# Attention block with adjacency mask on one core: exponentials issued behind each step's piece, half of the mask written by ScalarE, the last tail in halves

## The chip, the cores and the metric

One of the eight cores of a Trainium2 chip. The time is device microseconds of the slowest (here the only) core. Kernels are compared by the ratio to runs of the kernel before on the same chip.

In the profile's lines PE is TensorE (matrix products), PEld its weight loads, DVE is VectorE, ACT ScalarE, POOL GpSimd and SP SyncE. The kernels put TensorE's results into tiles of their PSUM pools, here called banks; an accumulating DMA is a transfer that a kernel issues with accum_op=ALU.add, to add to what stands at its target. A line of a wait list says who waited, in which line of the kernel, for whom: us in all, times, longest. One fp32 matmul of the program is two in the profile's counts (the values' four matmuls a step are 8192 records in 1024 steps); a transpose is one (four of them are an x4).

## The reference, cut to what matters

```python
# x: (8, 2048, 256) fp32; adj: (2048, 2048) int32, about 0.8% ones; H = 8 heads of D = 32
q, k, v = split(x @ w_qkv)                       # per frame f
scores = einsum("fnhd,fmhd->fhnm", q, k) / sqrt(32)
scores = where(adj > 0, scores, -1e9)
t = softmax(scores) @ v
y = layernorm(x + t) ; y = layernorm(y + relu(y @ w1 + b1) @ w2 + b2)   # with gains and shifts
out = layernorm(x + y)
```

## The kernel before

The loop has 1024 steps: 8 frames, 4 query blocks of 512, 2 groups of 4 heads, 16 key blocks of 128. A step makes the scores of the step two ahead (four 32-row matmuls side by side), VectorE adds the mask while copying them out of PSUM, ScalarE takes the exponential, and TensorE multiplies the current step's exponentials with the values.

```python
for t, (f, qc, g, mb) in enumerate(items):
    ...
    if mb:
        advance(t, 1)                    # one "piece" of other work that needs a PSUM bank
    scores(items[t + 2])                 # TensorE, then two VectorE additions
    values(items[t])                     # TensorE
    exponentials(items[t + 2])           # ScalarE, 128x2048
    add_up(items[t])                     # sums of exponentials: GpSimd or accumulating DMAs
```

Everything else (turning x, projections, closing sums, norms and the feed-forward of blocks already finished) is cut into pieces, at most one a step. The kernel uses eight banks of PSUM: six hold score pairs, one collects the group's output, and one is left for all pieces:

```python
def bank(...):
    if state["side"] is not None:
        return ps_x[1 - state["side"]].tile(...)      # in the loop: always the same one
    ...                                               # outside: five to choose from

def turn_rows(xc, xT):
    for a in range(2):
        yield BANK                                    # waits for the next step
        ps = bank()
        ... four transposes into ps
        nc.scalar.copy(xT[:, a, :], ps)               # ScalarE, behind exponentials(t + 1)
```

The masks are made before the loop: VectorE casts a chunk of adj to 0 or -57344, TensorE transposes it, VectorE writes it as fp8 in two halves. After the loop, the last block's sums, division, norms and feed-forward run alone.

## Time and profile before

| | us |
|---|---|
| median of the runs beside the changed kernel | 3594.7 (3592.2 to 3596.2) |
| start of the loop (masks, first projections) | 99.9 |
| loop, from its first scores to the end of the last values | 3417.4 |
| tail | 73.5 |
| TensorE idle in the loop | 304.1 |

The three stages are read from the records: the loop starts at the first scores after the mask stage and ends with the last values matmul.

### The profile page before, as it was taken

How to read it: one execution, taken by the hardware profiler on the slowest of the kernel's cores; microseconds unless marked ns; L12 is line 12 of the kernel's file. 1: busy time of each engine (PE TensorE's matmuls, PEld its weight loads, DVE VectorE, ACT ScalarE, POOL GpSimd, SP SyncE). 2: the span in 40 equal slices, each digit the busy share in tenths (PEclk: the TensorE clock that was granted, in tenths of full speed). 3: DMA queues.
4: the chain of work that ended last, by engine and by line, in shares of the span. 5: the costliest groups of instructions: out<-in, count | busy, mean ns of one | idle time of the engine just before them, and what ended most of it. 6: DMA issues, size and time to landing. Idle time of an engine off the chain costs nothing. (4 is left out here: it accounts for less than half of the span.)

```text
span 3590.9 us, 54434 instructions
## 1 busy us (share of the span) xinstructions
PE 3199.5 (89%) x22020; PEld 1036.2 (29%) x22020; DVE 2745.6 (76%) x3191; ACT 2413.7 (67%) x1921; POOL 2628.5 (73%) x1399
## 2 busy tenths in 40 slices
PE   6889998899988999998989999999998999988884
PEld 4222332223322233222322223222232223322221
DVE  5788768886788867877778776887768877688882
ACT  2576667776677766777677676677667776677772
POOL 3577768787688766878677776787767877688885
PEclk8999999999999999999999999999999999999997
DMA  8677768778578767778667778677776778587763
GB/s 300 138 157 159 171 149 179 153 152 187 130 158 188 154 155 154 155 165 186 156 143 163 158 159 183 131 165 172 156 178 144 151 163 176 137 170 161 152 143 73
DMA packets 146226, 576.52 MB, mean 161 GB/s; under 512 B 14608, under 2 KB 63248, under 8 KB 96816
## 3 DMA queue, kind: packets, MB, share of 16 engines
q0 software_dynamic: 66960, 443.19, 61.0%
q1 hardware_dynamic: 78192, 128.48, 10.5%
q8 instruction: 174, 2.85, 0.3%
q10 hardware_dynamic: 816, 1.31, 0.1%
q14 instruction: 84, 0.69, 0.1%
HBM read 132.52 MB, written 37.75 MB: 47 GB/s over the span
## 5 line engine op out<-in xcount | busy, mean ns | idle before, releaser
L213 DVE TENSOR_TENSOR p<-s,mask 128x1024 f32<-128x1024 f32 x2048 | 2410.2, 1219 | 697.8 <-PE s L210 409.0
L217 ACT ACTIVATE p<-p 128x2048 f32<-128x2048 f32 x1024 | 1957.4, 1911 | 1059.0 <-DVE p L213 820.4
L249 POOL TENSOR_TENSOR p<-p 128x2048 f32<-128x2048 f32 x384 | 1858.4, 4888 | 423.6 <-ACT p L217 421.6
L210 PE MATMUL s<-qT,kT 32*128 32x512 f32 x8192 | 1171.0, 641 | 169.3 <-DVE p L213 165.1
L229 PE MATMUL x<-p,v 128*32 128x512 f32 x8192 | 1092.9, 606 | 0.0
L246 POOL DMA_DIRECT2D p<-p x384 | 385.3, 1022 | 362.3 <-ACT p L217 149.9
L210 PEld LDWEIGHTS s<-qT,kT 32*128 32x128 f32 x8192 | 320.3, 183 | 797.9 <-DVE p L213 648.5
L229 PEld LDWEIGHTS x<-p,v 128*32 128x32 f32 x8192 | 161.3, 108 | 778.5 <-issue 544.1
L267 ACT ACTIVATE y<-y,nb,rs 128x256 f32<-128x256 f32 x384 | 224.9, 589 | 37.8 <-POOL nb L264 37.8
L283 PE MATMUL x<-p,ones 128*32 128x512 f32 x2048 | 243.9, 594 | 2.7 <-POOL p L249 1.2
L167 PE MATMUL x<-in,wqkv 128*128 128x512 f32 x472 | 234.0, 618 | 13.8 <-ACT turned L331 7.8
L256 DVE BATCH_NORM_STATS2 st<-y 128x6 f32<-128x256 f32 x384 | 160.0, 417 | 24.9 <-DMA y<-in_x_dram 24.9
L341 PE MATMUL x<-turned,w1s 128*128 128x512 f32 x256 | 130.6, 633 | 21.3 <-ACT hT L342 20.4
L167 PEld LDWEIGHTS x<-in,wqkv 128*128 128x128 f32 x472 | 79.9, 189 | 174.2 <-issue 71.7
L351 PE MATMUL x<-w2s,hT 128*128 128x256 f32 x512 | 127.6, 392 | 2.6 <-ACT hT L342 1.8
L192 PE MATMUL x<-wqkv,in 128*128 128x128 f32 x896 | 114.9, 281 | 7.2 <-ACT kT L169 7.0
L192 PEld LDWEIGHTS x<-wqkv,in 128*128 128x128 f32 x896 | 104.2, 191 | 55.9 <-ACT kT L169 38.3
L351 PEld LDWEIGHTS x<-w2s,hT 128*128 128x128 f32 x512 | 92.0, 189 | 66.6 <-ACT hT L342 29.4
L283 PEld LDWEIGHTS x<-p,ones 128*32 128x32 f32 x2048 | 63.4, 110 | 163.7 <-issue 124.4
L261 POOL TENSOR_TENSOR rs<-rs,mhalf 128x4 f32<-128x4 f32 x96 | 99.5, 1036 | 8.0
L330 PE MATMUL x<-ident,y 128*128 128x128 f32 x256 | 47.7, 297 | 53.2 <-ACT turned L331 37.7
L358 POOL TENSOR_TENSOR y<-y,be2r 128x1024 f32<-128x1024 f32 x32 | 94.2, 2943 | 0.2
(89 smaller groups left out, 1401.0 us busy)
## 6 DMA issues: line engine op xcount, KB each, us to landing
p<-p POOLq DMA_DIRECT2D x384, 1024.0 KB, 9.8
y<-in_x_dram POOLq DMA_DIRECT2D x64, 512.0 KB, 6.2
mask<-md SPq DMA_DIRECT2D x248, 128.0 KB, 5.7
in<-xd SPq DMA_DIRECT2D x59, 512.0 KB, 7.3
p<-in_adj_dram SPq DMA_DIRECT2D x16, 1024.0 KB, 15.4
out_dram<-y SPq DMA_DIRECT2D x32, 512.0 KB, 4.7
in<-in_x_dram SPq DMA_DIRECT2D x28, 512.0 KB, 5.6
xd<-in SPq DMA_DIRECT2D x28, 512.0 KB, 8.9
```

What stands on the lines that cost most here:

```text
L167: nc.tensor.matmul(ps, wqkv[:, a, k0:k0 + P], xT[:, a, :], start=(a == 0), stop=(a == 1))
L192: nc.tensor.matmul(ps[:, j * P:(j + 1) * P], xT[:, a, j * P:(j + 1) * P], wqkv[:, a, 2 * C + g * P:2 * C + (g + 1) * P], start=(a == 0), s ...
L210: nc.tensor.matmul(ps2[half][:, j, :], KT[f, mb // TPC, g][r:r + D, (mb % TPC) * P:(mb % TPC + 1) * P], QT[f, qc, g][r:r + D, :], start=Tr ...
L213: nc.vector.tensor_tensor(pt[:, 2 * half:2 * half + 2, :], ps, MK[f, qc, mb // 2][:, mb % 2, None, :].to_broadcast([P, 2, CH]), ALU.add)
L217: nc.scalar.activation(PT[item], PT[item], AF.Exp, scale=1.0 / math.sqrt(D))
L229: nc.tensor.matmul(O[grp][r:r + D, :], V[f, mb // TPC, g][:, mb % TPC, r:r + D], PT[item][:, h, :], start=(mb == 0), stop=(mb == LAST))
L246: nc.gpsimd.dma_start(PT[f, qc, g, chain[0]], PT.pop(item), accum_op=ALU.add)
L249: nc.gpsimd.tensor_tensor(first, first, PT.pop(item), ALU.add)
L256: nc.vector.bn_stats(st, t[:, j, :])
L267: nc.scalar.activation(t[:, j, :], t[:, j, :], AF.Identity, bias=nb[:, j:j + 1], scale=rs[:, j:j + 1])
L283: nc.tensor.matmul(ps[r:r + D, :], cst["ones"], term[:, h, :], start=(n == 0), stop=(n == 3))
L351: nc.tensor.matmul(ps[:, (j - jj) * C:(j - jj + 1) * C], hT[:, d, j * P:(j + 1) * P], w2s[:, d, :], start=(d == 0), stop=(d == 1))
```

## The change

It has three parts. The exponential of the next step is issued after this step's piece and before the scores, so that the copy that empties the pieces' bank stands ahead of it in ScalarE's queue. ScalarE writes half of each mask chunk. The last block gets its own tail: it works in halves, adds x by VectorE and not by DMA, may use five banks, and its last two tiles of exponentials go into the closing sum on TensorE and not through GpSimd. Besides, the stores of the masks and of the first turned x are issued by SyncE and no longer by GpSimd.

```diff
-            nc.vector.tensor_tensor(m, ps, ones, ALU.min, saturate=False)
-            nc.gpsimd.dma_start(MD[qc, k], words(m))
+            if half:
+                nc.vector.tensor_tensor(m, ps, ones, ALU.min, saturate=False)
+            else:
+                nc.scalar.copy(m.bitcast(I8), ps)         # -5 as int8 is -57344 as fp8
+            nc.sync.dma_start(MD[qc, k], words(m))
...
-            nc.vector.tensor_scalar(cv, col, 0.0, MASKED, op0=ALU.is_le, op1=ALU.mult)
+            for half, what in enumerate((CODE, MASKED)):
+                ... the same on half of the columns
...
         if mb:
             advance(t, 1)
+        if t + 1 < len(items):
+            exponentials(items[t + 1])
         ... scores(items[t + LEAD])
         values(items[t])
-        if t + LEAD < len(items):
-            exponentials(items[t + LEAD])
         add_up(items[t])
...
+    ENDED = (13, 15)                  # of the last group: not added by GpSimd, but terms of the sum
+    def finish(f, qc):                # the last block's tail
+        yield from divide(f, qc, y)
+        nc.vector.tensor_tensor(y, y, xr, ALU.add)        # x loaded 8 steps before the end
+        norm_halves(y) ; ... feed_forward(y) ; norm_halves(z)
+        ... gain and shift + x by VectorE, in halves
+        norm_halves(z) ; two output DMAs
...
     t = len(items)
+    state["side"] = None              # five banks from here on
```

More of the change, by code (lines that the diff above doesn't have):

```diff
@@ L13 @@
 I32 = mybir.dt.int32
+I8 = mybir.dt.int8
 F8 = mybir.dt.float8e5
@@ L31 @@
 MASKED = -57344.0
+CODE = -5.0
 BIG = 2.0 ** 64
@@ L126, in mask_blocks @@
             m = to[half] if to else mask_piece(0, qc, k)
-            nc.vector.tensor_tensor(m, ps, cst["ones"][:, 0:1, None].to_broadcast([P, 2, CH]), ALU.min, saturate=False)
-            nc.gpsimd.dma_start(MD[qc, k], words(m))
+            if half:
+                nc.vector.tensor_tensor(m, ps, cst["ones"][:, 0:1, None].to_broadcast([P, 2, CH]), ALU.min, saturate=False)
+            else:
+                nc.scalar.copy(m.bitcast(I8), ps)
+            nc.sync.dma_start(MD[qc, k], words(m))
     def load_mask(f, qc, k):
@@ L246, in add_up @@
                 nc.gpsimd.dma_start(PT[f, qc, g, chain[0]], PT.pop(item), accum_op=ALU.add)
-        if mb in POOLED[1:]:
+        if mb in POOLED[1:] and not ((f, qc, g) == items[-1][:3] and mb in ENDED):
             first = PT[f, qc, g, POOLED[0]]
@@ L275, in denominator @@
         terms = [PT.pop((f, qc, g, ALONE))] + [PT.pop((f, qc, g, chain[0])) for chain in MOVED + (POOLED,)]
+        if (f, qc, g) == items[-1][:3]:
+            terms[3:3] = [PT.pop((f, qc, g, b)) for b in ENDED]
         yield BANK
@@ L282, in denominator @@
                 r = D * h
-                nc.tensor.matmul(ps[r:r + D, :], cst["ones"], term[:, h, :], start=(n == 0), stop=(n == 3))
+                nc.tensor.matmul(ps[r:r + D, :], cst["ones"], term[:, h, :], start=(n == 0), stop=(n == len(terms) - 1))
         dT = op.tile([P, CH], F32, name="dT")
@@ L299, in denominator @@
             begin = items.index((f, qc, g, LAST)) + SUM + 2
-            start(begin, outcome(f, qc), begin)
+            start(begin, outcome(f, qc) if (f, qc) != (F - 1, NCK - 1) else finish(f, qc), begin)
     def outcome(f, qc):
@@ L304, in outcome, with divide @@
         state["tails"] += 1
-        rc = RC.pop((f, qc))
         xin = x[f, qc * CH:(qc + 1) * CH, :].rearrange("(p j) c -> p j c", p=P)
         y = yp.tile([P, TPC, C], F32, name="y")
+        yield from divide(f, qc, y)
+        nc.gpsimd.dma_start(y, xin, accum_op=ALU.add)
+        begin = items.index((f, qc, 1, LAST)) + SUM + 2
+        start(begin + 10, tail(f, qc, y, xin), begin + 26)
+    def divide(f, qc, y):
+        rc = RC.pop((f, qc))
         for gg in range(2):
@@ L316, in outcome @@
                                     rc[:, :, 4 * gg:4 * gg + 4, None].to_broadcast([P, TPC, 4, D]), ALU.mult)
-        nc.gpsimd.dma_start(y, xin, accum_op=ALU.add)
-        begin = items.index((f, qc, 1, LAST)) + SUM + 2
-        start(begin + 10, tail(f, qc, y, xin), begin + 26)
     def tail(f, qc, y, xin):
         yield from norm(y)
+        yield from feed_forward(y)
+        yield 1
+        z = y
+        yield from norm(z)
+        nc.gpsimd.tensor_tensor(z, z, rows(cst["g2r"]), ALU.mult)
@@ new lines, in tail, with norm_halves @@
+        yield 1
+        nc.gpsimd.tensor_tensor(z, z, rows(cst["be2r"]), ALU.add)
+        yield 1
+        nc.gpsimd.dma_start(z, xin, accum_op=ALU.add)
+        yield 7
+        yield from norm(z)
+        nc.sync.dma_start(out[f, qc * CH:(qc + 1) * CH, :].rearrange("(p j) c -> p j c", p=P), z)
+        state["tails"] -= 1
+    def norm_halves(t):
+        both = []
+        for h in range(0, TPC, 2):
+            mv = small.tile([P, 2, nc.vector.BN_AGGR_DIM], F32, name="mv")
+            for j in range(2):
+                st = small.tile([P, nc.vector.BN_STATS_DIM], F32, name="st")
+                nc.vector.bn_stats(st, t[:, h + j, :])
+                nc.vector.bn_aggr(mv[:, j, :], st)
+            rs = small.tile([P, 2], F32, name="rs")
+            nc.gpsimd.tensor_scalar(rs, mv[:, :, 1], EPS, 1.0, op0=ALU.add, op1=ALU.mult)
+            nc.gpsimd.tensor_tensor(rs, rs, cst["mhalf"][:, 0:2], ALU.pow)
+            nb = small.tile([P, 2], F32, name="nb")
+            nc.vector.scalar_tensor_tensor(nb, mv[:, :, 0], -1.0, rs, op0=ALU.mult, op1=ALU.mult)
+            both.append((h, rs, nb))
+        for h, rs, nb in both:
+            for j in range(2):
+                nc.scalar.activation(t[:, h + j, :], t[:, h + j, :], AF.Identity, bias=nb[:, j:j + 1], scale=rs[:, j:j + 1])
@@ new lines, in finish @@
+    def finish(f, qc):
+        y = yp.tile([P, TPC, C], F32, name="y")
+        xr, xb = state["rows"], take([P, TPC, C], F32)
+        yield from divide(f, qc, y)
+        nc.vector.tensor_tensor(y, y, xr, ALU.add)
+        norm_halves(y)
+        nc.vector.tensor_tensor(xb, xr, rows(cst["be2r"]), ALU.add)
+        yield from feed_forward(y)
+        z = y
+        norm_halves(z)
+        for h in range(0, TPC, 2):
+            nc.vector.tensor_tensor(z[:, h:h + 2], z[:, h:h + 2], rows(cst["g2r"])[:, h:h + 2], ALU.mult)
+            nc.vector.tensor_tensor(z[:, h:h + 2], z[:, h:h + 2], xb[:, h:h + 2], ALU.add)
+        norm_halves(z)
+        dst = out[f, qc * CH:(qc + 1) * CH, :].rearrange("(p j) c -> p j c", p=P)
+        for h in range(0, TPC, 2):
+            nc.sync.dma_start(dst[:, h:h + 2], z[:, h:h + 2])
@@ L323, in tail, with feed_forward @@
+    def feed_forward(y):
         yield TURNED
@@ L353, in tail @@
             nc.vector.tensor_tensor(z[:, jj:jj + 2, :], ps.rearrange("p (b c) -> p b c", c=C), z[:, jj:jj + 2, :], ALU.add)
-        yield 1
-        yield from norm(z)
-        nc.gpsimd.tensor_tensor(z, z, rows(cst["g2r"]), ALU.mult)
-        yield 1
-        nc.gpsimd.tensor_tensor(z, z, rows(cst["be2r"]), ALU.add)
-        yield 1
-        nc.gpsimd.dma_start(z, xin, accum_op=ALU.add)
-        yield 7
-        yield from norm(z)
-        nc.sync.dma_start(out[f, qc * CH:(qc + 1) * CH, :].rearrange("(p j) c -> p j c", p=P), z)
-        state["tails"] -= 1
     fill = []
@@ L425, in begin @@
             cv = two[:, c % 2 * TPC * CH:(c % 2 + 1) * TPC * CH].rearrange("p (j m) -> p j m", m=CH)
-            nc.vector.tensor_scalar(cv, col, 0.0, MASKED, op0=ALU.is_le, op1=ALU.mult)
+            for half, what in enumerate((CODE, MASKED)):
+                part = slice(half * 2 * P, (half + 1) * 2 * P)
+                nc.vector.tensor_scalar(cv[:, :, part], col[:, :, part], 0.0, what, op0=ALU.is_le, op1=ALU.mult)
             fetch()
@@ L430, in begin @@
                 yield from turn_rows(rows[c][:, 0:2, :].rearrange("p a (b c) -> p (a b) c", c=C), xT)
-                nc.gpsimd.dma_start(XD[0][c], xT)
+                nc.sync.dma_start(XD[0][c], xT)
                 XT[0, c] = xT
@@ L444, in begin @@
                     scores(items[k])
-                    exponentials(items[k])
+                exponentials(items[0])
     def ask(f, c):
@@ L465, in fast_path @@
                 start(t, what(f + 1, *which), due)
+        if t == len(items) - MB // 2:
+            state["rows"] = take([P, TPC, C], F32)
+            nc.sync.dma_start(state["rows"], x[f, qc * CH:(qc + 1) * CH, :].rearrange("(p j) c -> p j c", p=P))
         if mb:
             advance(t, 1)
+        if t + 1 < len(items):
+            exponentials(items[t + 1])
         if t + LEAD < len(items):
```

## The prediction

> **What bounds the kernel now.** I read the page's busy table first, then busy time by stage, then TensorE's waits inside the main loop, then the timeline of a stretch where it waits, and last the two ends. The table names TensorE, and the stage table (core: length, then busy us and instruction count of PE, PEld, DVE, ACT, POOL, then clock, DMA share, GB/s) says where it isn't bound:
>
> ```profile
> PE 3199.5 (89%) x22020; PEld 1036.2 (29%) x22020; DVE 2745.6 (76%) x3191; ACT 2413.7 (67%) x1921; POOL 2628.5 (73%) x1399
> ...
> 0.00:100.00 100.00, 63.42 (x476) 47.65 (x476) 60.96 (x53) 20.06 (x29) 31.97 (x54) 0.80 0.76 280
> 100.00:3518.00 3418.00, 3113.93 (x21463) 978.40 (x21464) 2670.02 (x3084) 2379.72 (x1867) 2565.70 (x1315) 1.00 0.73 160
> 3518.00:3591.00 73.00, 22.15 (x86) 10.12 (x85) 14.58 (x54) 13.88 (x26) 30.82 (x31) 0.66 0.19 45
> ```
>
> So there is a start of 100 us (the masks), a loop of 3418 us with 1024 steps in which TensorE is busy 91%, and a tail of 73 us. A loop step is: one "piece" of other work (a projection, a transpose, a part of the tail of an earlier block), the scores two steps ahead, then this step's values. The wait list of TensorE from 150 to 3500 us accounts for almost all of its 298 us of idle time there (3350 us less 3051 busy); columns are total us, times, longest:
>
> ```profile
> PE s L210 <- DVE p L213: 160.2, 347, 1.1
> PE x L147 <- ACT in L148: 40.9, 28, 2.0
> PE x L330 <- ACT turned L331: 36.5, 30, 1.4
> PE x L341 <- ACT hT L342: 19.0, 30, 1.0
> PE x L290 <- ACT dT L285: 16.0, 63, 0.5
> PE x L167 <- ACT turned L331: 7.8, 13, 0.7
> ```
>
> The first line is the steps without a piece: two score-plus-mask additions of VectorE (1.22 us each) take longer than scores plus values (1.14 + 1.06 us). All the others are one thing: a piece waits until ScalarE has copied the previous piece out of the only bank that pieces have. With four smaller ScalarE lines (7.0, 3.8, 3.2, 0.3) they sum to 134.5 us. The timeline shows why the copy is late (start us, length us, engine, line, what):
>
> ```profile
> 1907.06 0.81 PE L330 MATMUL x<-ident,y 128*128 128x128 f32 x4
> ...
> 1908.59 1.91 ACT L217 ACTIVATE p<-p 128x2048 f32<-128x2048 f32 x1 [1.10 <-DVE p L213]
> 1908.88 1.06 PE L229 MATMUL x<-p,v 128*32 128x512 f32 x8
> ...
> 1910.41 0.76 ACT L331 ACTIVATE turned<-x,be1c,g1c 128x512 f32<-128x512 f32 x1
> 1911.22 0.66 PE L330 MATMUL x<-ident,y 128*128 128x128 f32 x4 [1.28 <-ACT turned L331]
> ```
>
> The first transposes end at 1907.87, but ScalarE stands before an exponential that can only start at 1908.59 (it waits for VectorE) and lasts 1.91 us. The copy starts at 1910.41, 2.5 us after its data; TensorE loses 1.28 us.
>
> At the two ends, the second half of the mask stage and the chain of work that ended last:
>
> ```profile
> 72.09 1.22 DVE L426 TENSOR_SCALAR p<-p 128x2048 bf16<-128x2048 int32 x1
> 73.36 1.89 PE L124 MATMUL s<-identb,p 128*128 128x128 bf16 x16 [2.73 <-DVE p L426]
> 74.43 2.36 DVE L127 TENSOR_TENSOR in<-s,ones 128x1024 fp8e5<-128x1024 bf16 x2 [1.13 <-PE s L124]
> 76.71 1.22 DVE L426 TENSOR_SCALAR p<-p 128x2048 bf16<-128x2048 int32 x1
> ```
>
> ```profile
> 3519.48 4.55 POOL p L249
> 3530.73 5.54 DMA y<-in_x_dram
> 3572.16 5.58 DMA y<-in_x_dram
> ```
>
> One mask chunk takes 4.61 us, all of it VectorE (1.22 + 2.36) and a 1.13 us wait for the transposes. The tail is one serial chain with two accumulating DMAs in it.
>
> [...]
>
> **The change, part by part.**
>
> *Exponentials.* The step used to issue piece, scores(t+2), values(t), exp(t+2); now piece, exp(t+1), scores(t+2), values(t). The order listing of the built kernels confirms that on ScalarE each copy now stands before an exponential instead of behind it. No work is added or removed in the loop. In the example the copy would run at about 1907.9 to 1908.7, long before TensorE wants the bank at 1909.9. So up to 134.5 us go. I checked from the records whether VectorE lets TensorE use it: in the 219 steps with such a wait, I took the time from the end of the addition that frees the score bank to the start of the scores, less the wait: 0.82 us on average, 0.17 after the turn transposes, 0.26 after the tail's transposes, 1.56 after the feed-forward. Nearly every wait is recoverable. I take off 20 us for three things: transposes in the same step as a normalization put 0.76 + 0.59 + 1.91 = 3.26 us on ScalarE in a step of 0.66 + 1.14 + 1.06 less overlap, about 2.8 us, with some 1 us of slack before the values; GpSimd, already 75% busy in the loop, holds p buffers, and VectorE's additions already wait 33 us for buffers (behind GpSimd and DMA); and a norm's scale from GpSimd now has one exponential less to hide behind (in the loop only 3 of the norms would have been late, 2.4 us in all). Gain 115 us.
>
> *Masks.* The cast is cut into two of 128x1024, so about 0.65 us each; the first half is copied by ScalarE (about 1.05 us, from 0.59 for 512 elements), leaving one 1.22 us VectorE operation of two. Chain per chunk: 0.65 cast, then both transposes at the slow clock (1.89), 0.1 latency, 1.22 last VectorE op: about 3.9 us in place of 4.61. Over the last 8 chunks that is 5.6 us; the first 8 are held by TensorE, ScalarE copies and adjacency loads and gain little. I take 5 us. The DMAs moved to SyncE's queue are off the path.
>
> *Tail* (T is the last values' end, 3517.3). Two GpSimd additions of 4.55 us leave the chain, but 16 sum matmuls of 0.12 us come in and all 48 run after the last feed-forward piece: 2.0 + 48 x 0.116 = T+7.6, against T+7.8 before. No gain. From there: with five banks to choose from, reciprocal and both divisions end at about T+11.4 (T+12.8 before), and x is added from SBUF by an addition of 1.22 us instead of a DMA: T+12.9 with the queue's small operations, against T+19.0, gain 6.1. First norm and feed-forward: halves start ScalarE earlier and the copies no longer wait for banks (0.8 to 0.9 us, three times), but the matmuls stay at the slow clock: 21.7 us in place of 24.5, gain 2.8. Second norm, gain and shift: 4.5 + 4 x 0.69 = 7.3 us in place of 17.0 (two 2.34 us GpSimd operations and a 6 us DMA), gain 9.7. Last norm: finished after 5.7 us, but the order listing puts the previous block's last norm behind it on VectorE, GpSimd and ScalarE: 4.4 + 2.1 + 2.1 + 2.1 = 10.8 us to the end of ScalarE, against 6.3 before: loss 4.5. Sum 14 us.
>
> Total 115 + 5 + 14 = 134 us: 3595 - 134 = 3461 us.
>
> **Rivals.** (1) The wait moves to values waiting for exponentials, since exp(t+1) now stands behind a copy that waits for its piece. For it: in steps without a piece, values start only 0.99 us after their exponential ends, at the least 0.20. Against: after a piece with a copy there were 1.7 to 3.6 us on average. It would cost 30 to 60 us: about 3505. (2) VectorE becomes the bound and eats the gain, since its wait is already the largest. Against: the slack above. It would leave half: about 3525. (3) GpSimd or its accumulating DMAs (9.8 us to landing) hold buffers longer than the shorter steps allow. GpSimd would go from 75 to 78%; it sits idle 406 us waiting for exponentials. 10 to 30 us: about 3480. (4) Everything is recovered, and the clock stays up in the tail: about 3435.
>
> **Range and chances.** Rivals 1 and 3 in part give the upper end, 3505; full recovery the lower, 3435. Within 2% means above 3523, which needs the loop's gain to be less than about half; slower would need a new wait that the trace gives no hint of.
>
> **What would show it.** Right: TensorE's waits on ScalarE in the loop shrink from 134 us to under 20, its busy time in the loop stays near 3114 us, its wait on VectorE stays near 160 to 180 us, the mask chunk takes about 3.9 us, no DMA of x in the final chain, and the last ScalarE work belongs to the older block's norm. Wrong: a new line of values waiting for the exponential, or VectorE's wait growing by what ScalarE's lost, or VectorE's additions waiting for GpSimd for far more than 33 us.

## More of the kernel before

"Half clock" is a granted TensorE clock of 0.50 in the trace, full clock one of 1.00.

## The result

The changed kernel took 3439.9 us (3433.6 to 3453.0, four runs) against 3594.7, ratio 0.9575 with an interval of 0.9546 to 0.9603: 155 us won where 134 were forecast, inside the range. A ratio is the mean time of one kernel's fast runs over that of the other's of the same rounds, so it is not quite the ratio of the medians quoted.

The busy table and the three stages of the changed kernel (core: length, then busy us and count of PE, PEld, DVE, ACT, POOL, clock, DMA share, GB/s):

```profile
PE 3179.1 (92%) x22036; PEld 1038.5 (30%) x22036; DVE 2731.0 (79%) x3203; ACT 2426.5 (71%) x1937; POOL 2586.7 (75%) x1357
...
0.00:92.84 92.84, 63.45 (x472) 47.83 (x472) 43.85 (x53) 34.37 (x45) 6.75 (x19) 0.83 0.82 291
92.84:3385.61 3292.77, 3094.87 (x21460) 979.91 (x21460) 2666.88 (x3084) 2377.57 (x1867) 2561.08 (x1313) 1.00 0.76 166
3385.61:3440.00 54.39, 20.75 (x106) 10.80 (x104) 20.26 (x67) 14.56 (x26) 18.82 (x25) 0.75 0.19 45
```

| | before | after | won | forecast |
|---|---|---|---|---|
| start | 99.9 | 92.8 | 7.1 | 5 |
| loop | 3417.4 | 3292.8 | 124.6 | 115 |
| tail | 73.5 | 53.5 | 20.0 | 14 |

The stages are those of the two profiled executions, which lie 151.8 us apart; the medians lie 154.8 us apart.

**The loop.** What TensorE waits for in the loop of the changed kernel, whole list (total us, times, longest):

```profile
PE s L215 <- DVE p L218: 173.2, 358, 1.5
PE x L172 <- DMA in<-xd: 14.1, 8, 3.1
PE x L234 <- ACT p L222: 2.3, 2, 1.7
PE s L215 <- DVE in L130: 1.3, 1, 1.3
PE x L172 <- ACT turned L395: 0.3, 1, 0.3
```

Every wait of a piece for a ScalarE copy is gone but 0.3 us. The wait for VectorE has grown from 163.8 us (same bounds) to 173.2, and one of 1.2 us has become 14.1: projections that wait for reloaded inputs. TensorE's idle time fell by 106.2 us, from 304.1 to 197.9 (length less busy, both loops). The other 18.4 us of the 124.6 are busy time: 3113.3 before, 3094.9 after, for the same matmuls. (TensorE ran at half clock for two stretches of 3.41 us in the loop before and for one after; I estimate that this is 1.6 of the 18.4 us, from a later run with five more such stretches and 8.1 us more of busy time.) The timeline of two transpose pieces, as in the stretch shown of before:

```profile
1829.46 0.66 PE L394 MATMUL x<-ident,y 128*128 128x128 f32 x4
...
1830.28 0.76 ACT L395 ACTIVATE turned<-x,be1c,g1c 128x512 f32<-128x512 f32 x1
...
1830.99 1.91 ACT L222 ACTIVATE p<-p 128x2048 f32<-128x2048 f32 x1
...
1832.11 0.66 PE L394 MATMUL x<-ident,y 128*128 128x128 f32 x4
```

The copy starts at 1830.28, 0.16 us after its transposes end at 1830.12, and the exponential follows it. The next transposes start without a wait; the two pieces are 2.65 us apart, where they were 4.16 us apart before.

**The start.** One mask chunk of the second half:

```profile
69.69 1.29 DVE L482 TENSOR_SCALAR p<-p 128x1024 bf16<-128x1024 int32 x2
...
70.43 1.89 PE L126 MATMUL s<-identb,p 128*128 128x128 bf16 x16 [1.92 <-DVE p L482]
71.54 1.01 ACT L132 CAST in<-s 128x1024 int8<-128x1024 bf16 x1 [2.84 <-PE s L126]
72.41 1.23 DVE L130 TENSOR_TENSOR in<-s,ones 128x1024 fp8e5<-128x1024 bf16 x1 [1.44 <-issue]
...
73.55 0.68 DVE L482 TENSOR_SCALAR p<-p 128x1024 bf16<-128x1024 int32 x1
```

The transposes start 0.74 us into the cast instead of 1.27 us, take 1.89 us as before (at half clock in both: from 59.3 to 103.6 us before, from 60.9 to 98.5 after), ScalarE's copy runs beside them, and one VectorE operation is left behind them: 3.86 us a chunk instead of 4.61.

**The tail.** Some of its lines, from the last block's sums to the end:

```profile
3391.51 3.64 PE L292 MATMUL x<-p,ones 128*32 128x512 f32 x32 [1.91 <-DMA p<-p]
...
3398.53 1.22 DVE L372 TENSOR_TENSOR y<-y,in 128x1024 f32<-128x1024 f32 x1
...
3407.07 4.83 PE L405 MATMUL s<-turned,w1s 128*128 128x512 f32 x8
...
3433.08 2.07 ACT L274 ACTIVATE y<-y,nb,rs 128x256 f32<-128x256 f32 x4 [2.99 <-POOL nb L271]
```

The sums wait 1.91 us for an accumulating DMA; x is added by VectorE in 1.22 us, what its score additions of the same size took in the loop before (1.219 us on average); the first layer of the feed-forward takes 4.83 us for eight matmuls (7.6 before, in two lots of 3.79 us); and the last work of the kernel is the previous block's norm. GpSimd's power operation in a norm takes 0.70 us for the 2 columns of a half, 1.03 us for 4.

### The profile page after: what moved, and what is told of

Same layout as the page of the kernel before.

```text
span 3439.1 us, 54435 instructions
## 1 busy us (share of the span) xinstructions
PE 3179.1 (92%) x22036; PEld 1038.5 (30%) x22036; DVE 2731.0 (79%) x3203; ACT 2426.5 (71%) x1937; POOL 2586.7 (75%) x1357
## 5 line engine op out<-in xcount | busy, mean ns | idle before, releaser
L172 PE MATMUL x<-in,wqkv 128*128 128x512 f32 x472 | 235.2, 621 | 14.7 <-DMA in<-xd 14.1
L294 ACT COPY dT<-x 128x512 f32<-128x512 f32 x64 | 37.4, 585 | 126.3 <-PE x L292 126.3
L405 PE MATMUL x<-turned,w1s 128*128 128x512 f32 x248 | 123.0, 618 | 0.0
L200 ACT COPY v<-x 128x512 f32<-128x512 f32 x58 | 33.9, 585 | 93.6 <-PE x L197 93.6
## 6 DMA issues: line engine op xcount, KB each, us to landing
p<-p POOLq DMA_DIRECT2D x384, 1024.0 KB, 10.1
in<-xd SPq DMA_DIRECT2D x59, 512.0 KB, 10.9
in<-in_x_dram SPq DMA_DIRECT2D x29, 512.0 KB, 10.4
```

Source lines behind the costliest of these rows:

```text
L172: nc.tensor.matmul(ps, wqkv[:, a, k0:k0 + P], xT[:, a, :], start=(a == 0), stop=(a == 1))
L405: nc.tensor.matmul(ps, w1s[:, a, d * P:(d + 1) * P], yT[:, a, :], start=(a == 0), stop=(a == 1))
```

## The experiments

Twelve runs, on chips 15, 7 and 12; in all three the kernel before took about 3600 us (medians 3600.1, 3598.4, 3600.1). The changed kernel run again:

> The changed kernel itself, as the reference on this chip for the runs beside it. 0.957 of the kernel before, 3440 to 3446 us, as first measured.

It took 3444.0 us, ratio 0.9566 (0.9553 to 0.9579), as expected.

### The exponentials alone, and all but the exponentials

The first kernel is the one before with two edits: the `exponentials` call moved as in the change, and only the first of the two opening exponentials issued before the loop.

> The kernel before with nothing changed but the place of the exponentials (issued behind the step's piece, one step later). Theory: the whole loop gain comes from the copies standing ahead of an exponential, so this part alone gives what the loop gained in the full change, 3417.4 - 3292.8 = 124.6 us: about 3470 us, ratio 0.965, TensorE's waits on ScalarE in the loop under 10 us (134.5 before), its wait on VectorE 165 to 180 us. Rival: part of the loop's gain comes from the other edits (fewer DMAs on GpSimd's queue, another start of the loop): then 3485 us or more. Rival 2: the new 14 us wait for reloaded inputs comes from the mask stores that moved to SyncE's queue: then it is absent here and the time is about 3456 us.

The second is the changed kernel with that edit undone.

> The changed kernel with the exponentials back in their old place; masks and tail as changed. Theory: parts add up, start 7 us and tail 20 us stay: about 3567 us, ratio 0.9925, waits on ScalarE in the loop back at about 134 us. Rival: the tail's gain depends on the faster loop before it (TensorE's clock, the older block's norm): then 3575 us or more.

Alone it took 3480.4 us, ratio 0.9677 (0.9663 to 0.9692); undone, 3570.8 us, ratio 0.9920 (0.9904 to 0.9935). The two parts won 3.2% and 0.8% and together 4.0%, against 4.25 to 4.3% for the full change. By the medians that is 119.7 + 29.3 = 149.0 us against 154.4: they nearly add up, and the rest isn't settled, since the full change was not timed beside them. The first took 10 us more than its theory said and lies between that and the first rival (3485). What speaks against that rival is the loop: it took 3298.0 us, 119.4 of the 124.6 us that the full change won there, and the loop of the changed kernel itself took 3292.8, 3291.3 and 3300.2 us in three profiles (the last with useless transposes added in the tail). The second kernel's loop took 3420.6 us. TensorE's waits in the loop of the first from 110 to 3395 us, whole list, and the largest wait on ScalarE in the second's, as before (all of them sum to 137.1 us, 136.5 before):

```profile
PE s L210 <- DVE p L213: 174.2, 357, 2.3
PE x L167 <- DMA in<-xd: 16.9, 7, 3.5
PE x L229 <- ACT p L217: 1.2, 1, 1.2
```

```profile
PE x L152 <- ACT in L153: 41.0, 28, 2.0
```

So the order of the exponentials alone takes the waits on ScalarE away and alone brings the wait for reloads: the moved mask stores have no part in that (the second rival falls). In the second kernel the tail took 52.8 us, so the tail's gain doesn't depend on the faster loop either.

### The masks alone

> The kernel before with the mask part alone (casts in halves, ScalarE copies one half, stores from SyncE). Theory: one mask chunk of the second half takes 3.8 us in place of 4.6, the loop starts 7 us earlier, all else as before: 0.998, 7 us. Rival: the stores on SyncE hold up adjacency loads behind them and give some of it back: 3 us or less.

3589.1 us, ratio 0.9969 (0.9960 to 0.9978): 11 us (8 to 14 by the interval), more than the 7 expected. The loop started at 96.7 us; in the kernel of the next section, which ran beside it with the old mask stage, it started at 104.7, so the stage itself won 8.0 us. The remaining 3 us are within that interval and have no cause that I can show; the tail, unchanged, took 70.4 us here and 76.5 there.

### Is it the bank, or ScalarE's load?

If TensorE waits because the copy stands behind an exponential, then a copy made by another engine must remove that wait in the kernel before. The first attempt changed the helper that turns rows:

```diff
-            nc.scalar.copy(xT[:, a, :], ps)
+            nc.vector.tensor_copy(xT[:, a, :], ps)
```

> The kernel before, exponentials in their old place, but the copies of the turned rows (56 in the loop) made by VectorE in place of ScalarE. Theory: what TensorE waited for was a bank whose copy stood behind an exponential, not ScalarE's work as such: with the copy on an engine that has no exponential in its queue the wait of the turn transposes on the copy falls from 40.9 us to under 8 while all the other waits on ScalarE (94 us) stay, and the time falls by 20 to 40 us: ratio 0.989 to 0.994. Rival: the bank is not the cause, and pieces wait anyway (on VectorE now, whose queue is full too): same time, within 10 us.

3607.6 us, ratio 1.0025 (1.0017 to 1.0034): a miss. But the helper also serves the start, where VectorE's copies came to stand behind casts that wait for the adjacency loads: the loop started at 126.4 us, some 22 to 27 us late. The loop itself took 3404.0 us. So it was run again with VectorE's copies in the loop alone:

> The kernel before with the copies of turned rows on VectorE in the loop alone (the earlier run moved those of the start too, where they stood behind casts that wait for the adjacency loads, and the start grew by 26 us). Theory: as in that run's loop, the turn transposes' wait for their copy goes (40.9 us to 0.5), the next piece's wait for the query copy grows (3 to 20 us): 13 to 20 us are won, ratio 0.994 to 0.996. Rival: no gain at all, VectorE's two-input additions lose what TensorE wins.

3588.7 us, ratio 0.9967 (0.9954 to 0.9979): 11 us won, a little under the 13 to 20 expected; loop 3407.1 us against 3419.5 of the kernel with the masks alone beside it. The two largest of TensorE's waits on ScalarE from 110 to 3500 us:

```profile
PE x L330 <- ACT turned L331: 39.9, 31, 1.4
PE x L167 <- ACT qT L169: 19.2, 28, 0.8
```

The turn transposes' own wait, 40.9 us, fell to 0.6. The 28 query projections that follow them now wait for the next copy on ScalarE instead, 19.2 us in place of 3.2: removing one link, 40.3 us, moves 16.0 of them to the next link of the same kind, since that copy still stands behind an exponential. The order change moves all links at once. So the cause is where the copy that frees the bank stands in ScalarE's queue. ScalarE's total work is not: it was busy for 2379.1 us in the loop before and for 2377.6 after. That the waits also need the single bank is argued: no run gave the pieces a second one.

### GpSimd's last two additions

```diff
-    ENDED = (13, 15)
+    ENDED = ()
```

> The changed kernel, but GpSimd adds the last two tiles (blocks 13 and 15 of the last group) as before, so the closing sum has 4 terms and not 6. Theory of the prediction: that part gains nothing, because in the changed kernel the sums wait for the accumulating DMA of block 12 and then run 32 matmuls of 0.12 us: sums end 9.5 us after the last values; here GpSimd's two additions (4.6 us each) end at about +8.5 to +9.5 and 8 matmuls follow: +9.5 to +10.5. Span 3438 to 3442 us. Rival: the additions are on the chain, and leaving them out won 4 to 9 us: sums end at +14 or later, span 3443 to 3448 us.

A single run: 3452.1 us. Its loop was longer, 3301.9 us, mostly because TensorE ran at half clock six times there for 3.4 us, once in the changed kernel: busy time was 3103.0 us, not 3094.9. So only the tail is compared. The last sums ended 8.0 us after the last values and the tail took 51.9 us, against 9.5 and 53.5 in the changed kernel (54.7 in its second run):

```profile
3402.91 1.06 PE L292 MATMUL x<-p,ones 128*32 128x512 f32 x8 [0.71 <-DMA p<-p]
...
3405.34 1.06 PE L292 MATMUL x<-p,ones 128*32 128x512 f32 x8 [1.37 <-POOL p L256]
```

The sums wait 0.7 us for the DMA and 1.4 us for GpSimd, then eight matmuls end them. That part of the change won nothing, as predicted. In a later kernel with the same edit the sums ended at +10.4 us, with the last eight matmuls at half clock (1.91 us, not 1.06), so the 1.5 us are within the scatter, not a loss.

### The new wait for reloads

```diff
         nc.sync.dma_start(xT, XD[f][c])
-        yield 3
+        yield 5
```

> The changed kernel with 5 steps in place of 3 between the issue of a reloaded input and its first use. Theory: the new wait of TensorE for reloaded inputs (14.1 us, 8 times) is a fixed lead of 3 steps that has become too short now that steps last 3.2 and not 3.3 us and the reload lands after 10.9 us (median) and not 7.3: the wait falls under 3 us and the time to about 3428 us. Rival: the reload waits for a free buffer or for its own store, so a longer lead only moves the wait: same time, 3440 us, and inputs held longer.

3434.6 us (3428 expected), ratio 0.9539 (0.9526 to 0.9552), and the wait is gone from the list. Together with GpSimd's additions, five rounds beside the changed kernel:

> The changed kernel with the 5-step reload lead and with GpSimd adding blocks 13 and 15. Theory: the two add up, 13 us from the reload wait and 1.5 us from the sums: 0.953 of the kernel before, about 15 us under the changed kernel beside it. Rival: no better than the reload change alone.

3433.3 us, ratio 0.9537 (0.9524 to 0.9550), 11 us under the changed kernel's 3444.0 of the same rounds. That is no better than the longer lead alone: the rival held, as GpSimd's additions win and lose nothing. The lead of 3 steps had become too short, less because steps are shorter than because reloads land later: 10.9 us (median) after their issue, 7.3 before. The same holds for loads of x, 10.4 against 5.6 us, and only in kernels with the new order (10.1 with the order alone, 5.4 with it undone). From the records, the number of accumulating DMAs under way while a load of x was under way was 0.45 on average before and 1.07 after. The new order moves GpSimd's accumulations against the loads in time; whether it is they that make the loads land later was not shown, since no run tried it by itself. For the reloads the new order is not the only way there: with the turn copies on VectorE and the old order they also landed after 10.6 us (median), and TensorE waited for them for 5.4 us in all.

### TensorE's clock in the tail

The prediction had the tail's matmuls at half clock, as they were before (four 512-column matmuls of the first layer took 3.79 us there, at 0.50, and 1.98 us in the loop). In the changed kernel the two stretches around the feed-forward's first layer have these clocks (the number before the DMA share):

```profile
3399.80:3407.00 7.20, 2.70 (x8) 1.48 (x8) 3.55 (x13) 3.43 (x7) 1.79 (x4) 0.69 0.00 0
3407.00:3412.00 5.00, 4.99 (x11) 2.27 (x10) 0.00 (x0) 2.90 (x7) 4.73 (x3) 0.76 0.00 0
```

The clock fell for 6.8 us and came back in the third matmul (1.22, 1.06, 0.82 us, then 0.59 five times). Before, it was down for 23.9 us, and all eight matmuls took 1.06 or 1.22. Can it be kept up?

```diff
         yield from divide(f, qc, y)
+        yield BANK
+        ps = bank()
+        for n in range(40):
+            nc.tensor.transpose(ps[:, n % 4 * P:(n % 4 + 1) * P], ident, ident)
```

> The changed kernel with 40 transposes of no use on TensorE while VectorE and GpSimd make the last block's first norm. Theory: what the prediction had wrong in the tail is the clock: in the changed kernel TensorE's clock falls to half for 6.8 us only, and the feed-forward's first two and a half matmuls pay for it (1.22, 1.06, 0.82 us, then 0.59). Kept busy it doesn't fall: all eight near 0.59, feed-forward's two layers in 3.5 us (4.8 in the changed kernel), transposes faster too, and the tail 1 to 2.5 us shorter than 53.5. Rival: the transposes of no use delay the real ones: tail the same or longer.

No. The tail took 54.9 us. The 40 transposes ended at 3414.5 us, and the clock had been full to there; the next two stretches are the real transposes and the first layer:

```profile
3415.00:3419.00 4.00, 1.87 (x7) 1.20 (x8) 2.05 (x6) 2.73 (x6) 0.89 (x2) 0.83 0.00 0
3419.00:3426.00 7.00, 6.98 (x13) 2.91 (x11) 0.00 (x0) 3.14 (x6) 6.27 (x3) 0.61 0.00 0
```

The clock stayed up during the 40 transposes and fell 3.2 us after they ended, when TensorE had done only two more transposes, of 0.33 us each, so that more of the first layer was slow (6.1 us for its eight matmuls). The loss was only put off. In the second run of the changed kernel the clock was down for 10.2 us and five matmuls were slow: the depth of this loss varies from run to run by a few us.

The traces also show when the clock falls. Its changes lie on a grid of 3.41 us. The loops of all fourteen traces, cut at that grid, have 13592 such windows at full clock. The clock fell after 72 of them, and in these TensorE was busy for 49% of the window or less; in the 13520 others it was busy for 43% or more. In the kernel before the clock fell after two windows, both busy for 43%, in the changed kernel after one, busy for 11%; the 1957 others of these two loops were busy for 47% or more.

### Filling the steps without a piece

What is left is the wait for VectorE in 357 steps without a piece. They last 2.63 us on average in the changed kernel, though TensorE needs only about 2.1 us of work there (2.63 less 173.2 us of wait over 358 times). If that is right, cutting long pieces in two or four and spreading them fills such steps for nothing. The closing sum of each group (32 matmuls in two steps) was spread over four; while a bank is half filled, no other piece may start:

```diff
-            if n == 2:
-                yield BANK
+            if n:
+                yield MORE                     # next part of the same bank
...
-                if e[2] == BANK:
-                    if not banks:
+                if e[2] in (BANK, MORE):
+                    if not banks or state["mid"] not in (None, e):
                         break
```

> The same, and each group's closing sum (16 + 16 matmuls in two steps) spread over four steps of 8. Theory: what is left of TensorE's idle time in the loop, 173 us, is the 357 steps without a piece, each losing 0.42 to 0.48 us to VectorE's two additions; 126 of them get a piece, so the wait on VectorE falls to 110 to 125 us and the time by 50 us, to 0.939 of the kernel before. Rival: a step with a 0.9 us piece is short enough for VectorE's norm statistics (0.6 us) to bind it, so half is lost: 25 us, 0.946. Rival 2: pieces stand in each other's way with the bank held for four steps: no gain.

3349.1 us, ratio 0.9305 (0.9293 to 0.9318): 84 us under its own base, more than expected. Steps without a piece fell from 357 to 231, and the wait for VectorE in the loop from 175.8 to 111.8 us. The loop got 80.3 us shorter: 64.8 us of TensorE's idle time and again 15.5 us of its busy time (3093.3 to 3077.8 for the same matmuls). Both times that pauses were removed, busy time fell with them: 18.4 us with 190 fewer waits for pieces (0.10 us each), 15.5 us with 126 fewer (0.12 us each). In both pairs the first kernel had one stretch of half clock more, which is 1.6 us by the same estimate. Why busy time falls with the pauses is not shown. This version beats both kernels.

Then the same for the projections of queries and keys (two halves each), with the rule that a split piece may not straddle the end of a group. Both edits are in one kernel:

> The version with sums in four, and the projections of queries and keys (118 in the loop, two 512-column matmuls of 1 us each) also spread over two steps, the bank held between them. The built order has 162 steps without a piece, 231 before. Theory: each step that gets a piece saves 0.48 us of TensorE's wait on VectorE: 69 x 0.48 = 33 us, so 0.921 of the kernel before, wait on VectorE 75 to 85 us. Rival: the schedule is crowded at the change of frames, where the built order now forces several pieces into one step (155 adjacent pieces, 120 before), and norms and reloads are pushed back: 10 to 20 us or nothing.

3630.3 us, ratio 1.0073 (1.0058 to 1.0089): slower than the kernel before. Two lines of VectorE's waits in its loop:

```profile
DVE p L219 <- DMA p<-p: 118.6, 52, 6.9
...
DVE st L264 <- DMA y<-in_x_dram: 81.8, 20, 5.1
```

VectorE's additions wait 118.6 us for tiles of exponentials still held by accumulating DMAs (3.8 us with the sums alone split), and 81.8 us at norms for x. Steps without a piece did fall, to 162, but they last 3.28 us now; and 14 times the closing sum, its transposes and a value projection, put off until nothing could wait, fell into one step, of 10.2 us on average. That pieces which come late hold the tiles that VectorE needs next is a reading of these waits; no run tried one of the two edits without the other. The rival was right, and worse than it was stated.

The waits cost a second time. The loop is 278.5 us longer than with the sums alone split; 174.2 us of that are idle time of TensorE, but 104.3 us are busy time, for the same matmuls. The granted clock is the number before the DMA share:

```profile
97.46:3574.20 3476.74, 3182.15 (x21460) 991.95 (x21460) 2674.14 (x3084) 2384.57 (x1867) 2560.07 (x1314) 0.97 0.72 157
```

The records have 43 falls to half clock in this loop, 204.8 us in all, and none in the loop with the sums alone split. TensorE was busy for 172.2 us of them. If matmuls take twice their time there, as the first layer's nearly do (1.06 us against 0.59), half of that, 86 us, is my estimate of what the clock cost; the rest of the 104.3 isn't settled. All six runs had this low clock (0.959 to 0.963 over the whole execution).

## Why the prediction was right or wrong

The mechanism and the size of the largest term were right; the total came out 21 us better than forecast, over three stages that were all underestimated (2.1, 9.6 and 6.0 us; the rest is the difference between the profiled executions and the medians).

**Exponentials.** "Up to 134.5 us go" held to within 0.3 us for the copies, shown by both kernels with that edit alone or undone. The deduction of 20 us had three reasons, and none was of that size. ScalarE's crowding cost 2.3 us of values waiting for exponentials. VectorE's additions waited 28.6 us behind GpSimd and accumulating DMAs, not more than the 32.9 us before (same bounds of the loop). The wait for VectorE grew by 9.4 us. What did come was not among the reasons: 14.1 us of waits for reloads. And the prediction said that busy time stays near 3114 us; it fell by 18.4. So the term was 124.6 us where 115 were forecast, with some luck: the idle time, which is all that the forecast counted, fell by 106.2 us, less than forecast, and the fall of busy time that nobody foresaw made up for it.

**Masks.** 3.86 us a chunk against 3.9: right. (The parts that the prediction names for the old chunk, 1.22 + 2.36 + 1.13, sum to 4.71; its 4.61 is the distance between casts, as VectorE's records overlap: one ends at 76.79 us, the next starts at 76.71.) Eight chunks give 6.0 us, the stage won 7.1 (8.0 with the masks alone).

**Tail.** Worked out in four links. Up to the sum with x: 14.2 us after the last values, not 12.9, because the sums waited for the DMA of block 12 (9.5 us, not 7.6); 4.9 us won, 6.1 forecast. First norm and feed-forward: 17.1 us, not 21.7; 7.4 won, 2.8 forecast. The step that failed most is "the matmuls stay at the slow clock": TensorE was idle for 5.4 us before the transposes, not 11.7, it had no pause from the third transpose on, where there were three of 0.8 to 0.9 us before, and the clock was back after 6.8 us. The first layer took 4.7 us up to the second, 7.6 before without its two pauses. Starting in halves was undersized too: the first transposes began 3.2 us after the norm's start, 4.9 before. Second norm, gain and shift: 7.3 us, as forecast (9.7 won); its four 128x512 operations on VectorE took 0.68 or 0.69 us each, as those of that size did in the kernel before (0.68 and 0.69 us on average). Last norm: ScalarE ended 11.0 us after its start, 10.8 forecast, behind the previous block's norm; but from there to the end of the kernel it took 4.0 us, 6.7 before, so 1.9 us were lost and not 4.5. Why the last store took less time isn't settled. That leaving out GpSimd's additions gains nothing was right.

**Rivals.** Values waiting for exponentials: 2.3 us, no. VectorE becoming the bound: its wait grew by 9.4 us, a small part. GpSimd: 78% busy in the loop, no wait of TensorE behind it. The optimistic one had the right total (3435), for other reasons than it gave in full: the clock came back in the tail, but not all was recovered in the loop.

## What to carry to other kernels

In ScalarE's queue, what stands ahead of a short copy mattered more than the engine's load. A copy with its data ready at 1907.87 us started at 1910.41, behind an exponential of 1.91 us; moving the exponentials alone made the loop 119.4 us shorter, while ScalarE was busy for 2379.1 us in the loop before and 2377.6 after the full change. So put the copy that frees a scarce bank ahead of the long operation that merely follows, and check in the built order that it stands there. Where one engine sets the pace of some steps and another that of the rest, count the steps of each kind and spread the filler over all of them (231 steps without a piece in place of 357 won 84 us), but stop before the filler is so late that it holds buffers that the loop needs (the last from one run, and argued). A long wait of TensorE can be paid for twice: in the last experiment the clock fell to half 43 times in the loop, which I estimate at 86 us of busy time, beside 174.2 us more of idle time. After a step gets shorter, look again at every prefetch whose lead is counted in steps: 3 steps of 3.2 us in place of 3.3 were too few for reloads that landed after 10.9 us in place of 7.3, and TensorE waited 14.1 us for them.
